# Two graph-attention layers on neighbour lists: layer 0's order on VectorE and GpSimd, its tile order, and where the prelude's transposes stand

## The chip, the cores and the metric

The kernel runs on one core of one Trainium2 chip. The metric is the device time of one execution in microseconds (us). The kernel before took 2356.4 us in the median of three runs (2355.76 to 2357.28). The profiled execution that all durations below come from took 2358.97 us, of which 2356.9 us is the span from the first to the last instruction. The engines are TensorE (PE, with its weight loads as PEld), VectorE (DVE), ScalarE (ACT), GpSimd (POOL) and SyncE (SP). Each works through its own queue in order.

## What is computed

Two graph layers over N = 2708 nodes with D = 1024 features, float32 throughout. `adj` is a symmetric 0/1 matrix with ones on the diagonal, of which a row has some 16 ones in the mean.

```python
# layer 0
f, g   = x @ Wf + bf, x @ Wg + bg
e      = relu(f @ g.T)
att    = softmax(where(adj > 0, e, -9e15), axis=1)
x      = layernorm(x + att @ (x @ W + bW))
# layer 1
h      = x @ W1
e      = leaky_relu(h @ a1 + (h @ a2).T, 0.2)
att    = softmax(where(adj > 0, e, -9e15), axis=1)
x      = layernorm(x + relu(att @ h))
```

## The kernel before

**Lists in place of the matrix.** Only the neighbours of a node enter its softmax. So the kernel first turns each row of `adj` into a list of at most 40 neighbours. It sorts the nodes by the length of their lists, in steps of four, and then works on 85 groups of 32 nodes. A group has a fixed number of tiles (`TILES`, 10 for the first and 3 for the last ones, 405 in all). In a tile each of the 128 partitions holds the feature row of one neighbour: partition 32q + i belongs to node i of the group, and q runs over four neighbours. Four groups make a block of 128 nodes, and there are 22 blocks (b0 to b21). If the lists were longer than the tiles allow, a second, dense path at the end would run (`general_path`); with these inputs it is skipped.

**Algebra.** Layer 0 doesn't form g. With M = Wf Wg^T, F = x M + c is formed for each block, and a score is the dot product of a row of F with a neighbour's row of x, plus a term q of the node itself. After the softmax the rows of x are summed (`sums`, PSUM tile `po`), scaled to y, and only then multiplied by W (`Wt`). The residual x is gathered into z, added, and normalised (`norm`). Layer 1's scores need two numbers a row, which layer 0 forms by two dots with u1b and u2b (the "u dots") when it closes a block. The row, with the second number, is scattered to a table T1 (rows of 1028 floats), and stored to X1S.

**Prelude.** For each of 22 row blocks `lists(b)` loads `adj` (1.35 MB, SP queue, pool `adjp`, four buffers), converts it on ScalarE, multiplies it by a descending index on GpSimd, and takes the largest elements on VectorE (`max`, `match_replace`). Between these, the generator `weights()` loads rows of Wf, Wg and W1 (pool `stage`, five buffers), transposes them on TensorE (`turned`), copies them out of PSUM on ScalarE, and forms M in two halves of 512 columns, then rb (for q) and u1b, u2b. Each `next(steps)` runs it up to the next `yield`, one row block of a weight. The calls after `lists(1)`, `lists(2)` and `lists(3)` run 16 of the 24 steps; the eight for W1 come after all lists. All this is in order on each engine's queue. Then the lists' lengths are ranked with VectorE and TensorE, which yields `idq` and `ids`, the indices of list rows and of x rows.

**Layer 0.** It is written out by hand in the order of the queues: `InOrder` ties each engine's instructions to the order of the program text, and records them all at L53, its own line. A `Unit` is the tiles handled at a time. A block whose tiles fit the ring of 20 slots of 128 x 1024 floats is one unit (b5 to b21: 20 tiles each in b5 to b11, 16 in b12 to b18, 12 in b19 and b20, 3 in b21); b0 to b4 have two units of two groups each. For a unit u and the next one:

1. `replicate` copies rows of F for the next block out of PSUM to all four quarters of a tile Fr (ScalarE, four copies a group).
2. `sums(u)`: TensorE forms the softmax denominators (`pt<-rs,stack`) and then `po`, tile after tile in order of t. Each tile that is done frees a ring slot, and `gathers()` then issues, on GpSimd, the gathers of later tiles as long as their slots are free, strictly in the order of `u.tiles`. Hooks within `sums` finish the close of an older block (its T1 scatter).
3. TensorE, in its order: the transposes of x for block b + 2 (`x_turn`), the product of y of block b - 1 with Wt (`Wp`), the product F of block b + 2 (`f_product`), and the transposes of y of block b.
4. GpSimd: the x rows of the residual (z) and of block b + 3 (`load_x`, one buffer xb), and four gathers of list rows.
5. VectorE: the `dots` of the next unit, one instruction for each tile as its row lands, the q dot of block b + 3 (`q_dot`, reads xb), the `soft` of the next unit (some 16 small instructions with one exp on ScalarE), and the first part of `close(b - 1)`: z added to the product, norm, and then the u dots.

For blocks of one unit (`u.only`) three quarters of the dots come first, then q_dot and the close up to the norm, then the last quarter, soft, and the u dots. `q_spread`, a matmul that spreads q over the partitions and its read on VectorE, stands in `sums`. PSUM tiles `pt` have two buffers, `pm` (Wp and F) two, `po` one. The tiles of a unit are in order of group in layer 0 (`cut(R0, False)`), in order of t in layer 1 (`cut(R1, True)`).

**Layer 1** gathers from T1 into 27 slots and needs no dots; it is otherwise alike.

Of the kernel before, what the change touches and what calls it, by code (L numbers as in the profile page):

```python
# [88 lines left out]
def listed_path(ctx, tc, x, adj, Wf, bf, Wg, bg, W, bW, W1, a1, a2, out):  # L89
# [74 lines left out]
    with tc.tile_pool(name="pre", bufs=1) as pre:  # L164
# [41 lines left out]
        with tc.tile_pool(name="adjp", bufs=4) as adjp, tc.tile_pool(name="cands", bufs=2) as cands, \  # L206
                tc.tile_pool(name="wt", bufs=1) as wt, tc.tile_pool(name="stage", bufs=5) as stage:
# [23 lines left out]
            def weights():  # L231
# [17 lines left out]
                for k in range(KC):  # L249
                    turned(Wf, k, WfT[:, :, k * P:(k + 1) * P])  # L250
                    yield
                for h in range(H):
                    half = slice(h * 512, (h + 1) * 512)
                    WgT = wt.tile([P, KC, 512], F32, name="WgT")
                    for k in range(4):
                        turned(Wg, 4 * h + k, WgT[:, :, k * P:(k + 1) * P])
                        yield
                    for k in range(KC):
                        pm = ps_m.tile([P, H, 512], F32, name="pm")
                        for i in range(KC):  # L260
                            nc.tensor.matmul(pm[:, 0, :], WfT[:, i, k * P:(k + 1) * P], WgT[:, i, :],  # L261
                                             start=(i == 0), stop=(i == KC - 1))
                        nc.scalar.copy(M[:, k, half], pm[:, 0, :])  # L263

                    pm = ps_m.tile([P, H, 512], F32, name="pm")
                    for i in range(KC):
                        nc.tensor.matmul(pm[0:64, 0, :], bfc[:, i:i + 1].to_broadcast([P, 64]), WgT[:, i, :],
                                         start=(i == 0), stop=(i == KC - 1))
                        nc.tensor.matmul(pm[64:128, 0, :], bgc[:, i:i + 1].to_broadcast([P, 64]),
                                         WfT[:, i, half], start=(i == 0), stop=(i == KC - 1))  # L270
                    crow = pre.tile([1, 512], F32, name="crow")
                    nc.scalar.copy(crow, pm[0:1, 0, :])
                    row_parts(lambda t: nc.gpsimd.dma_start(t, crow.rearrange("o (p k) -> o p k", p=P)),
                              c3[:, half])
                    nc.scalar.copy(rb[64:128, half], pm[64:128, 0, :])
                    for q in range(2):
                        nc.scalar.copy(rb[32 * q:32 * q + 32, half], pm[64 + 32 * q:96 + 32 * q, 0, :])
                for h in range(H):
                    half = slice(h * 512, (h + 1) * 512)
                    W1T = wt.tile([P, KC, 512], F32, name="WgT")  # L280
                    for k in range(4):
                        turned(W1, 4 * h + k, W1T[:, :, k * P:(k + 1) * P])
                        yield

                    pm = ps_m.tile([P, H, 512], F32, name="pm")
                    for i in range(KC):
                        for j in range(2):
                            nc.tensor.matmul(pm[64 * j:64 * j + 64, 0, :],
                                             ac[:, i, j:j + 1].to_broadcast([P, 64]), W1T[:, i, :],
                                             start=(i == 0), stop=(i == KC - 1))  # L290
                    for j, u in enumerate((u1b, u2b)):
                        mine, other = 64 * j, 64 - 64 * j
                        nc.scalar.copy(u[mine:mine + 64, half], pm[mine:mine + 64, 0, :])
                        for q in (0, 32):
                            nc.scalar.copy(u[other + q:other + q + 32, half], pm[mine + q:mine + q + 32, 0, :])

# [36 lines left out]
            for b in range(NB):  # L333
                lists(b)
                for _ in range({1: 8, 2: 4, 3: 4}.get(b, 0)):
                    next(steps)
# [102 lines left out]
    def norm(z, n):  # L439
# [17 lines left out]
        dve.tensor_scalar(sh[:n], mv[:n, 0:1], r[:n], -1.0, op0=ALU.mult, op1=ALU.mult)  # L457
        act.activation(z[:n, :D], z[:n, :D], AF.Identity, bias=sh[:n], scale=r[:n])
# [4 lines left out]
    def cut(most, in_turn):  # L463


        units, at = [], 0
        for b in range(NB):
            gs = list(range(Q * b, min(Q * b + Q, NG)))
            whole = sum(TILES[g] for g in gs) <= most
            parts = [gs] if whole else [gs[:2], gs[2:]]  # L470
            for i, p in enumerate(parts):
                u = Unit()
                u.b, u.gs, u.at = b, p, at
                u.first, u.last, u.only = i == 0, i == len(parts) - 1, whole
                u.lo, u.hi = 32 * (p[0] - Q * b), 32 * (p[-1] - Q * b) + 32
                u.G, u.T = len(p), max(TILES[g] for g in p)
                u.tiles = [(k, g, t) for k, g in enumerate(p) for t in range(TILES[g])]
                if in_turn:
                    u.tiles.sort(key=lambda m: m[2])
                u.sc = scores[len(units) % 2][:, :u.G, :u.T]  # L480
                assert len(u.tiles) <= most
                at += len(u.tiles)
                units.append(u)
        return units

    class Layer:
# [16 lines left out]
        def gathers(self):  # L503
            while self.next < len(self.order) and (self.next < self.count or self.next - self.count in self.free):
# [27 lines left out]
        def sums(self, u, po, ahead, hooks):  # L532

# [8 lines left out]
            ahead()  # L542
# [39 lines left out]
    with ExitStack() as s0s:  # L582
# [4 lines left out]
        z = new_pool("zp", 1).tile([P, TW], F32, name="z")  # L587
        units = cut(R0, False)
        lay = Layer(units, [ring], D, x, stp)
        by_block = {b: [u for u in units if u.b == b] for b in range(NB)}  # L590
        xb, q, qd, F, Fr, xTs, yTs, Wp, y = {}, {}, {}, {}, {}, {}, {}, {}, {}
# [15 lines left out]
        def q_spread(b):  # L607
            n = nrows[b]
            pt = ps_t.tile([P, 4, P], F32, name="pt")
            pe.matmul(pt[:, 0, :Q], rep[:n], qd.pop(b)[:n], start=True, stop=True)  # L610
            q[b] = small.tile([P, Q], F32, name="q")
            dve.tensor_scalar(q[b], pt[:, 0, :Q], s0, None, op0=ALU.add)

        def x_turn(b):
            xTs[b] = tp.tile([P, KC, P], F32, name="xT")
            for _ in turn(xb.pop(b), nrows[b], xTs[b]):
# [21 lines left out]

        def close(b):

            n = nrows[b]
            dve.tensor_add(z[:n, :D], flat(Wp.pop(b))[:n], z[:n, :D])
            norm(z, n)
            m = nsize[b]
# [4 lines left out]
            yield  # L649
            scatter(T1[:, :], ids[:m, b:b + 1], z[:m])  # L650

        act.dma_start(Wt, W.rearrange("(k p) d -> p k d", p=P))
        load_lists(0)
        dve.tensor_scalar(SL0, SL[:, 0:Q, :], float(N - 1), None, op0=ALU.min)
        load_x(0)
        pool.memset(z[:, D:], 0.0)
# [3 lines left out]
        for b in (0, 1):  # L660
            q_dot(b)
            q_spread(b)
            x_turn(b)
            load_x(b + 1)
            f_product(b)
            if b == 0:
                for k in range(Q):
                    replicate(0, k)
        load_lists(3)
        dots(units[0], 0, len(units[0].tiles))  # L670
        q_dot(2)
        soft(units[0])
        closing = iter(())
        for k, u in enumerate(units):
# [11 lines left out]
            for r in reps[:3]:  # L686
                replicate(b + 1, r)
            lay.sums(u, po, lambda: q_spread(ahead) if u.first and ahead is not None else None,
                     {8: [lambda s=closing: [None for _ in s]]})
            closing = iter(())  # L690
            act.activation(y[b][u.lo:u.hi], flat(po)[u.lo:u.hi], AF.Copy, scale=u.ri[u.lo:u.hi])
            if u.first:
                if back is not None:
                    gather(pool, z[:nrows[back], :D], x, ids[:nrows[back], back:back + 1])
                if ahead is not None:
                    x_turn(ahead)
                if back is not None:
                    Wp[back] = product(nrows[back], yTs.pop(back)[0], Wt, 32)
# [11 lines left out]
            if u.first and b + 3 < NB:  # L710
                load_x(b + 3)
            if u.first and b + 4 < NB:
                load_lists(b + 4)
            count = len(nxt.tiles) if nxt is not None else 0
            part = count * 3 // 4 if u.only else count
            if nxt is not None:
                dots(nxt, 0, part)
            if u.last and b + 3 < NB:
                q_dot(b + 3)
            if nxt is not None and not u.only:  # L720
# [4 lines left out]
            if nxt is not None and u.only:  # L725
                dots(nxt, part, count)
                soft(nxt)
            if back is not None:
                next(closing)
        for _ in closing:  # L730
            pass
        b = NB - 1
        gather(pool, z[:nrows[b], :D], x, ids[:nrows[b], b:b + 1])
        for _ in yTs[b][1]:
            pass
        Wp[b] = product(nrows[b], yTs.pop(b)[0], Wt, 32)
        for _ in close(b):
# [3 lines left out]
    with ExitStack() as s1s:  # L741
# [5 lines left out]
        units = cut(R1, True)  # L747
# [30 lines left out]
        def close1(b):  # L778
# [5 lines left out]
            norm(z, m)  # L784
# [7 lines left out]
        for k, u in enumerate(units):  # L792
# [9 lines left out]
            lay.sums(u, po, lambda: None, {6: [lambda s=closing: [None for _ in s]]})  # L802
# [405 lines left out]
```

## Time and profile before

| stage | us | PE busy | DVE busy | ACT busy | POOL busy | DMA share | GB/s |
|---|---|---|---|---|---|---|---|
| prelude, 0 to 239 | 239 | 185.8 | 160.1 | 110.9 | 150.8 | 0.55 | 192 |
| start of layer 0, 239 to 318 | 79 | 38.6 | 29.6 | 20.1 | 40.5 | 0.48 | 166 |
| b0 to b4, two units each, 318 to 630 | 312 | 269.6 | 229.4 | 106.5 | 175.3 | 0.65 | 218 |
| b5 to b10, 20 tiles, 630 to 1001 | 371 | 262.2 | 220.1 | 123.4 | 180.3 | 0.55 | 185 |
| b11 to the end of layer 0, 1001 to 1573 | 572 | 433.8 | 307.3 | 195.7 | 231.3 | 0.48 | 164 |
| layer 1, 1573 to 2357 | 784 | 603.0 | 228.6 | 77.1 | 430.1 | 0.76 | 273 |
| profiled execution: span 2356.9, run 2358.97 | | 1793.0 | 1175.1 | 633.7 | 1208.3 | | |

The rows are stretches of the same span, so their lengths add up to it; the busy times are those within each stretch. A line of a timeline further down gives the start in us, the busy time in us, the engine, the line of the program (L53 is the helper that records the hand-written order), the operation, output<-input with their shapes, the count, and in brackets the idle time of the engine just before and what ended it. A line of the waits gives who waited for whom, the total in us, how many times, and the longest.

### The profile page before, as it was taken

The numbers are of one execution on the slowest core, as the hardware profiler recorded it, in microseconds if no ns is written. First come the engines' busy times: TensorE is split into PE (matmuls) and PEld (weight loads), VectorE is DVE, ScalarE is ACT, GpSimd is POOL, SyncE is SP. The second block draws the span as 40 slices with busy tenths as digits, with TensorE's granted clock in tenths as the row PEclk, the third lists the DMA queues.
The fourth block names the chain that finished last, engine by engine and source line by source line (L and its number), as shares of the span: only waits on it lengthen the run. The fifth ranks groups of instructions, "written<-read, shape, count | busy, mean of one in ns | idle before, by whom it ended". The sixth has DMA issues, their size and how long they took to land. (4 is left out here: it accounts for less than half of the span.)

```text
span 2356.9 us, 22380 instructions
## 1 busy us (share of the span) xinstructions
PE 1793.0 (76%) x6982; PEld 702.8 (30%) x6982; DVE 1175.1 (50%) x3615; ACT 633.7 (27%) x769; POOL 1208.3 (51%) x1173
## 2 busy tenths in 40 slices
PE   5987469999767776677777778835687888888896
PEld 3343223333222322223333333311222322333332
DVE  3994176777756666555655555321123323333333
ACT  4553322333423332234434333100001001111111
POOL 6891647555344444554555543026566656666521
PEclk8998689999888888888888889967899988899998
DMA  8561647766455555554555554338788989888830
GB/s 291 186 216 60 237 142 241 234 220 224 142 181 189 199 196 183 176 200 167 173 176 188 182 176 159 125 138 324 262 309 299 335 313 314 296 310 306 289 151 23
DMA packets 154201, 502.94 MB, mean 213 GB/s; under 512 B 36550, under 2 KB 36550, under 8 KB 151364
## 3 DMA queue, kind: packets, MB, share of 16 engines
q0 software_dynamic: 132160, 428.47, 52.4%
q1 hardware_dynamic: 13658, 68.30, 8.0%
q10 hardware_dynamic: 8254, 4.65, 0.7%
q8 instruction: 57, 0.93, 0.2%
q14 instruction: 72, 0.59, 0.1%
HBM read 509.64 MB, written 33.75 MB: 231 GB/s over the span
## 5 line engine op out<-in xcount | busy, mean ns | idle before, releaser
L53 POOL DMA_INDIRECT ring<-in_x_dram,SL x405 | 470.5, 1162 | 551.8 <-PE po L53 413.6
L53 DVE SCALAR_TENSOR_TENSOR j<-ring,Fr 128x1024 bf16<-128x1024 f32 x405 | 496.6, 1226 | 190.5 <-DMA ring<-in_x_dram,SL 156.5
L53 PE MATMUL po<-ring,st 128*32 128x512 f32 x2820 | 474.6, 676 | 3.0 <-issue 2.5
L53 POOL DMA_INDIRECT ring<-T,SL x300 | 298.6, 995 | 190.3 <-PE po L53 79.0
L53 PE MATMUL pm<-M,yT 128*128 128x512 f32 (+1 forms) x704 | 344.4, 626 | 57.2 <-issue 54.9
L53 ACT COPY Fr<-pm 32x1024 f32<-32x1024 f32 x340 | 341.1, 1003 | 21.0 <-issue 16.5
L53 PE MATMUL pm<-M,xT 128*128 128x512 f32 (+1 forms) x704 | 320.5, 607 | 8.7 <-issue 8.7
L53 PE MATMUL pm<-Wt,xT 128*128 128x512 f32 (+1 forms) x704 | 316.2, 602 | 6.4 <-ACT xT L53 6.4
L53 PE MATMUL pt<-rs,stack 128*32 128x1 f32 x340 | 13.2, 191 | 346.7 <-DVE rs L53 158.9
L53 PEld LDWEIGHTS po<-ring,st 128*32 128x32 f32 x2820 | 120.9, 123 | 304.3 <-issue 300.6
L53 PEld LDWEIGHTS pm<-M,yT 128*128 128x128 f32 (+1 forms) x704 | 131.8, 193 | 267.3 <-issue 266.7
L53 ACT ACTIVATE z<-z,sh,rstd 128x1024 f32<-128x1024 f32 (+2 forms) x44 | 54.3, 1235 | 580.3 <-DVE sh L53 564.8
L53 ACT ACTIVATE y<-po,ri 128x1024 f32<-128x1024 f32 (+2 forms) x50 | 55.6, 1112 | 574.2 <-remote 488.5
L53 PEld LDWEIGHTS pm<-M,xT 128*128 128x128 f32 (+1 forms) x704 | 129.5, 189 | 174.8 <-issue 174.8
L53 PEld LDWEIGHTS pm<-Wt,xT 128*128 128x128 f32 (+1 forms) x704 | 127.9, 187 | 168.0 <-issue 161.2
L53 DVE TENSOR_SCALAR scores<-ring,f1q 128x2 f32<-128x2 f32 (+6 forms) x105 | 24.6, 253 | 241.1 <-DMA ring<-T,SL 210.5
L53 POOL DMA_INDIRECT more<-T,SL x105 | 105.3, 1003 | 66.7 <-PE po L53 28.8
L310 POOL TENSOR_TENSOR adj<-adj,iota 128x2708 f32<-128x2708 f32 (+1 forms) x22 | 129.8, 5936 | 15.6 <-ACT adj L309 15.5
L53 DVE SCALAR_TENSOR_TENSOR j<-xb,rb 128x1024 bf16<-128x1024 f32 (+1 forms) x22 | 26.9, 1225 | 204.1 <-DMA xb<-in_x_dram,ids 141.0
L313 DVE MAX8 cand<-adj 128x8 f32<-128x136 f32 (+2 forms) x440 | 105.7, 284 | 30.8 <-POOL adj L310 30.8
L261 PE MATMUL pm<-WgT,WfT 128*128 128x512 f32 x256 | 116.0, 614 | 6.1 <-ACT M L263 3.8
L53 PEld LDWEIGHTS pt<-rs,stack 128*32 128x32 f32 x340 | 9.6, 126 | 361.9 <-ACT xT L53 252.8
(171 smaller groups left out, 1509.7 us busy)
## 6 DMA issues: line engine op xcount, KB each, us to landing
adj<-in_adj_dram SPq DMA_DIRECT2D x21, 1354.0 KB
X1S<-z SPq DMA_DIRECT2D x21, 512.0 KB
x<-X1S SPq DMA_DIRECT2D x21, 512.0 KB
ring<-in_x_dram,SL POOLq DMA_INDIRECT x405
ring<-T,SL POOLq DMA_INDIRECT x300
rows<-in_L_gnn_Wf_dram SPq DMA_DIRECT2D x8, 512.0 KB
rows<-in_L_gnn_Wg_dram SPq DMA_DIRECT2D x8, 512.0 KB
rows<-in_L_gnn_W_dram SPq DMA_DIRECT2D x8, 512.0 KB
```

Source lines behind the costliest of these rows:

```text
L53: made = self.tc.keep_in_program_order(op(*args, **kwargs))
L261: nc.tensor.matmul(pm[:, 0, :], WfT[:, i, k * P:(k + 1) * P], WgT[:, i, :], start=(i == 0), stop=(i == KC - 1))
L310: nc.gpsimd.tensor_tensor(k[:n], k[:n], iota[:n], op=ALU.mult)
L313: nc.vector.max(cand[:n, s, :], k[:n, s * SEG:min((s + 1) * SEG, N)])
```

## The change

In the prelude the transposes of Wg's second half and of W1's first half stand in the middle of the products for M (after k = 3) instead of after them, with two buffers for a transposed half (`halfT`); `adjp` goes from four buffers to three and `stage` from five to four; the weights' rows are requested earlier in SP's order.

```diff
-        with tc.tile_pool(name="adjp", bufs=4) as adjp, ...
-                tc.tile_pool(name="wt", bufs=1) as wt, tc.tile_pool(name="stage", bufs=5) as stage:
+        with tc.tile_pool(name="adjp", bufs=3) as adjp, ...
+                tc.tile_pool(name="wt", bufs=1) as wt, tc.tile_pool(name="stage", bufs=4) as stage:
...
+                def half_turned(w, h):
+                    t = wt.tile([P, KC, 512], F32, name="halfT", bufs=2)
+                    for k in range(4):
+                        turned(w, 4 * h + k, t[:, :, k * P:(k + 1) * P])
+                        yield
+                    return t
+                WgT = yield from half_turned(Wg, 0)
                 for h in range(H):
...
                         nc.scalar.copy(M[:, k, half], pm[:, 0, :])
+                        if k == 3:
+                            nxt = yield from half_turned(*((Wg, 1), (W1, 0))[h])
...
+                    if h == 0:
+                        W1T = yield from half_turned(W1, 1)
...
-                for _ in range({1: 8, 2: 4, 3: 4}.get(b, 0)):
+                for _ in range({0: 8, 1: 4, 2: 4, 8: 4, 15: 4}.get(b, 0)):
```

In layer 0 the tiles are sorted by t within pairs of groups; all dots of the next unit stand together, then soft, then the close up to the norm; the q dot, ScalarE's z and the u dots come at the beginning of the next turn, ahead of the next dots. The gather of xb goes before that of z; q_spread's matmul moves behind the Wt product, and its read on VectorE behind the dots. The last block's z goes to a free ring slot instead of the one z tile.

```diff
-                if in_turn:
-                    u.tiles.sort(key=lambda m: m[2])
+                u.tiles.sort(key=lambda m: (m[0] // turns, m[2]))
...
+        def load_residual(b):
+            z = zs if b + 1 < NB else lay.slots[lay.next % lay.count]
+            Z[b] = zs if b + 1 < NB else z[0][:, z[1], :]
+            gather(pool, Z[b][:nrows[b], :D], x, ids[:nrows[b], b:b + 1])
...
-            for r in reps[:3]:
+            for r in reps[:1]:
                 replicate(b + 1, r)
-            lay.sums(u, po, lambda: q_spread(ahead) if u.first and ahead is not None else None,
-                     {8: [lambda s=closing: [None for _ in s]]})
+            next(closing, None)
+            if loaded is not None:
+                q_dot(loaded)
+                loaded = None
+            next(closing, None)
+            for r in reps[1:3]:
+                replicate(b + 1, r)
+            lay.sums(u, po, {12: [lambda s=closing: [None for _ in s]]})
...
+            if u.first and ahead is not None:
+                x_turn(ahead)
+            if u.first and b + 3 < NB:
+                load_x(b + 3)
+                loaded = b + 3
+            if back is not None:
+                load_residual(back)
+                Wp[back] = product(nrows[back], yTs.pop(back)[0], Wt, 32)
+            spreading = iter(())
+            if u.first and ahead is not None:
+                spreading = q_spread(ahead)
+                next(spreading)
...
-            part = count * 3 // 4 if u.only else count
             if nxt is not None:
-                dots(nxt, 0, part)
-            if u.last and b + 3 < NB:
-                q_dot(b + 3)
-            if nxt is not None and not u.only:
+                dots(nxt, 0, len(nxt.tiles))
+            for _ in spreading:
+                pass
+            if nxt is not None:
                 soft(nxt)
             if back is not None:
                 closing = close(back)
                 next(closing)
-            if nxt is not None and u.only:
-                dots(nxt, part, count)
-                soft(nxt)
```

At the start of layer 0 the x rows of block 0 are gathered before the lists, eight ring gathers go before the x rows of block 1, only two groups of F are replicated before x of block 1 is turned, and the dots of the first unit come before the q dot of block 1.

```diff
         act.dma_start(Wt, W.rearrange("(k p) d -> p k d", p=P))
+        load_x(0)
         load_lists(0)
+        q_dot(0)
...
+        lay.gathers(8)
+        x_turn(0)
+        for _ in q_spread(0):
+            pass
+        load_x(1)
         lay.gathers()
...
+        f_product(0)
+        replicate(0, 0)
+        replicate(0, 1)
+        x_turn(1)
         load_lists(3)
+        f_product(1)
+        replicate(0, 2)
+        replicate(0, 3)
         dots(units[0], 0, len(units[0].tiles))
-        q_dot(2)
+        q_dot(1)
+        load_x(2)
+        for _ in q_spread(1):
+            pass
         soft(units[0])
```

Layer 1 calls the same helpers with `cut(R1, Q)`, which gives the order it had.

## The prediction

> **What bounds the kernel now.** I read the slices first, then the waits, then timelines of one block of each kind. Three stages: prelude (0 to 239 us), layer 0 (239 to 1573), layer 1 (1573 to 2357). In layer 1 the diff changes no order (all its units already sort by t, norm() is run through), so I leave its 784 us alone. The waits, in us in total, times, longest:
>
> ```profile
> PE pt L53 <- DVE rs L53: 158.9, 16, 16.7
> DVE j L53 <- DMA xb<-in_x_dram,ids: 141.0, 10, 36.6
> PE pt L53 <- ACT xT L53: 125.4, 11, 20.8
> DVE eq L359 <- PE pt L353: 28.6, 1, 28.6
> ```
>
> TensorE waits for a unit's softmax (rs, and the xT copy queued on ScalarE behind its exp), and VectorE for xb, the x rows of a later block that no dot of this block needs. In the prelude VectorE waits once for TensorE. A block of 20 tiles in one unit (b9 to b10) on TensorE, then VectorE:
>
> ```profile
> 873.08 0.29 PE L53 MATMUL pt<-rs,stack 128*32 128x1 f32 x8 [11.97 <-ACT xT L53]
> 915.49 1.04 PE L53 MATMUL pt<-ident,y 128*128 128x128 f32 x8
> 937.38 0.29 PE L53 MATMUL pt<-rs,stack 128*32 128x1 f32 x8 [20.85 <-ACT xT L53]
> ```
>
> ```profile
> 920.02 1.23 DVE L53 SCALAR_TENSOR_TENSOR j<-xb,rb 128x1024 bf16<-128x1024 f32 x1 [9.88 <-DMA xb<-in_x_dram,ids]
> 921.42 1.22 DVE L53 TENSOR_TENSOR z<-pm,z 128x1024 f32<-128x1024 f32 x1
> 927.05 0.21 DVE L53 TENSOR_SCALAR sh<-mv,rstd 128x1 f32<-128x1 f32 x1
> 927.18 1.22 DVE L53 SCALAR_TENSOR_TENSOR j<-ring,Fr 128x1024 bf16<-128x1024 f32 x1
> 933.51 0.18 DVE L53 TENSOR_TENSOR scores<-scores,q 128x20 f32<-128x20 f32 x1
> 937.06 0.17 DVE L53 TENSOR_REDUCE rs<-scores 128x4 f32<-128x20 f32 x1
> ```
>
> TensorE has done its block by 916.5 and idles 20.9 us. VectorE had 15 dots done at 910.1, waited 9.9 for xb, did q_dot (1.4) and the close of an older block (5.8), and only then the last 5 dots (6.3) and the softmax (3.9). Gathers could not start sooner: all 20 ring slots belong to this unit and come free as its sums run. The next block's on GpSimd, first, second, last:
>
> ```profile
> 942.01 0.99 POOL L53 DMA_INDIRECT ring<-in_x_dram,SL  x1 [21.87 <-PE po L53]
> 944.80 0.99 POOL L53 DMA_INDIRECT ring<-in_x_dram,SL  x1 [1.80 <-PE po L53]
> 975.68 0.99 POOL L53 DMA_INDIRECT ring<-in_x_dram,SL  x1 [0.30 <-issue]
> ```
>
> A 16-tile block is idle too, a two-unit block (b3) hardly:
>
> ```profile
> 1266.51 1.04 PE L53 MATMUL pt<-ident,y 128*128 128x128 f32 x8
> 1280.74 0.28 PE L53 MATMUL pt<-rs,stack 128*32 128x1 f32 x8 [13.19 <-DVE rs L53]
> ```
>
> ```profile
> 523.01 7.13 PE L53 MATMUL pm<-Wt,xT 128*128 128x512 f32 x16
> 530.08 0.23 PE L53 MATMUL pt<-rs,stack 128*32 128x1 f32 x4
> 560.40 0.23 PE L53 MATMUL pt<-rs,stack 128*32 128x1 f32 x4 [4.13 <-DVE rs L53]
> ```
>
> **The sum, against the profiled span of 2356.9 us** (0.5 above the median of the runs, 2356.4). Intervals run from rs matmul to rs matmul.
>
> *20-tile blocks, b5 to b11.* Six intervals, 629.92 to 1001.06, 61.9 each. Afterwards q_dot, the close and the two u dots stand after the softmax, ahead of the next dots: 5.8+1.4+2.5+0.2 = 9.9 us, and VectorE's old first dot came 9.4 after rs (946.76), when its row landed. So they hide behind the first gather. Twenty dots at 1.27 (25.4) then end at about 35, earlier than the gathers, which decide: 9.4 to the first landing, then 19 more and two 0.5 MB transfers among them, the T1 scatter and the X1S store, which formerly fell before the gathers. Pace: 975.68-949.19 over 16 issues is 1.66; ten landings in a row (dots at 952.46 to 970.67) give 1.82; I take 1.72. Sorting by pairs frees two slots per t step instead of one, which lets the queue fill sooner; since the transfers then set the pace I count nothing more for it. 9.4 + 21x1.72 + last dot 1.3 + q 0.2 + softmax 3.9 = 50.9. TensorE's own 43.7 (937.38 to 981.11) lies below. Six times -11.0 = **-66**. b11 to b12 has 16 gathers: 43.9, TensorE 43.7, with the hand-over 44.5 for 59.3: **-15**.
>
> *16-tile blocks.* 1060.37 to 1391.52, six intervals of 55.2, and 52.3 to b19. Four slots are spare, so 12 gathers and the two transfers remain: 9.4 + 13x1.72 + 5.2 = 37. TensorE's chain is longer: 40.6 from 1226.96 to the end of the y transposes. It would gain 1.3 in the sums if there is no gap before them (48 po matmuls took 7.46 after a gap of 10.35 us and 5.34 at 1483.16 without; 64 took 8.43 here), and lose some 0.9 where the second x transposes wait for a PSUM slot until ri, now queued behind the u dots, is read; hand-over 0.3. I take 41: six times -14.2 and -11.3 = **-96**. The TensorE page of the Trainium skill ("TensorE: Matmul & The Clock Gate", Part 1) has the array at half clock after an idle window of about 3.4 us; those two rows agree in direction, and by full speed alone the interval would be 39.6.
>
> *Two-unit blocks b1 to b4.* TensorE-bound: at 530.08 the second unit's rs was ready since 521.3. Afterwards the q matmul stands behind the Wt product, and q's read on VectorE ahead of the second unit's softmax. So softmax waits for Wt: 0.6 + 0.2 + 3.4 + hand-over, about 5 us of idle TensorE. The close and the u dots then start 5 later, the 12 dots and the softmax end at about 33.5 after the first rs + 30, TensorE at 31.5: 2 us idle in place of 4.5. Net +3 each, **+12** (0 to +24). b0 and the step to b5: **-2**.
>
> *Start of layer 0* (idq 238.5 to the first rs 317.6). load_x(0) now precedes the lists, so x lands at 244.1 (it took 4.5 from issue), F(0) ends at 263.3 instead of 270.0, and two replicate groups (8.1) instead of four (16.3) stand before the next work. The dots no longer wait for q_dot(1), whose xb landed at 288.07: they run from 271.5, not 290.7. SL0 comes 1.5 later, one xb gather more is among the ring's; rows are there long before. **-19** (-12 to -22).
>
> *End.* b20 to b21, 30.4: the close of b19 (waiting 13.4 for z) leaves the chain; TensorE's 5.3+14.8+1.0 and the copy give 22.8. From b21's rs to its T1 scatter, 56.6: z of the last block has a slot of its own and the Wt product no longer follows ScalarE's z (6.4): 7+14.8+0.7+1+14.5+10.4 = 48.7. **-15**.
>
> *Prelude.* TensorE ends it (228.1 against 199.8 on VectorE). The weight transposes between the products took 12.9 (115.7 to 128.6) and 10.8 (193.8 to 204.6), waiting mostly for ScalarE copies; inside M I estimate 8.5 and 4.5, as the copies still share ScalarE's queue with the adjacency blocks: -11. Wf's copies now run through before the second adjacency block: M starts some 7 earlier. VectorE has then 28.6 of slack to lose: adjp has three buffers, and on SP the last W1 rows wait for stage buffers that are freed by transposes in the middle of M, with blocks 16 to 21 queued behind. I put the lists' end at 205 instead of 196. **-18** (-24 to 0).
>
> Sum: -66-15-96+12-2-19-15-18 = -219, so a span of 2138 and a run at **2137 us**.
>
> **Rivals.**
> *Gathers faster.* If 1.30 (issue to issue, as from 973.06 to 978.27) is the pace, 20-tile blocks fall to TensorE's 44: another -41, 2096. Against: ten landings at 1.82. Chance 0.10.
> *Gathers slower.* 16-tile rows from 1182.02 to 1193.55 go at 1.92. Then 55 per 20-tile block, +25; others stay with TensorE: 2162. 0.13.
> *The close in front delays the block.* u dots wait for z on ScalarE, z for a replicate group (4.06); ri, the second x transposes and the dots wait behind. If a hand-over of 5 stays in each of 13 whole intervals: +65, 2202. For: the prelude and two-unit blocks show such in-order waits. Against: 9.4 us of gather latency as cover. 0.13.
> *VectorE holds up GpSimd.* If each gather issue waits for one dot, 0.99+1.23+0.30 = 2.52 a gather, 20-tile blocks grow to 67.7 and 16-tile ones become 47: about 2290. Against: from 484.74 to 489.92 five gathers beside unbroken dots take 0.99 each. 0.03. "SBUF — State Buffer" of the Trainium skill (Who interferes with whom) says so of a VectorE instruction with two SBUF inputs against a GpSimd one that reads SBUF; those rows speak against a price here.
> *Slower: transfers collide.* X1S, T1, z, xb and the ring's now fall into one shorter stretch. With p us a transfer, layer 0's whole intervals sum to 234p-610 against before and the rest to -42: no gain from p = 2.79, 2407 at 3.0. For: layer 0 never moved over 240 GB/s in 100 us. Against: layer 1's gathers run at 321 GB/s, 1.64 each. 0.04.
> *The prelude part does nothing*, as the lists take TensorE's place: 2155, inside the forecast's own range.
>
> **How the numbers follow.** Forecast 0.56, its own range 2108 to 2175. The range 2095 to 2202 takes in the faster and slower pace and half of the third rival. A difference under 0.2% (5 us) could not be told from none; only a sum of several rivals lands there, 0.01. Slower 0.04, faster 0.95.
>
> **What would show it.** In whole blocks j<-xb,rb after the softmax with no wait; 20-tile intervals near 51 with VectorE waiting for ring rows to the end; 16-tile ones near 41 with TensorE's gap before rs gone; in b1 to b4 a new TensorE gap of 5 us after Wt; eq's wait for pt below 10 us; layer 1 unchanged at 784. Wrong if the gap before rs stays over 10 us in 16-tile blocks, or if a gather takes over 2.5.

## The result and the profile after

The changed kernel took 2123.24 us in the median of four runs (2115.4 to 2125.75). The kernel before, run beside it, took 2356.08 (2349.6 to 2357.28). The ratio is 0.9011, 95% interval 0.8981 to 0.9041. The profiled run took 2115.4 us with a span of 2113.6, so all stages below add up to -243.3 against the profile of before (2356.9).

The waits of the changed kernel (who waited for whom, us in total, times, longest), those that answer to the ones shown of before:

```profile
PE pt L53 <- DVE rs L53: 36.5, 9, 5.6
PE pt L53 <- ACT xT L53: 24.1, 19, 11.7
DVE q L53 <- remote: 86.6, 10, 15.4
DVE j L53 <- DMA xb<-in_x_dram,ids: 5.7, 2, 5.5
DVE eq L365 <- PE pt L359: 1.1, 1, 1.1
```

TensorE's waits for the softmax have gone from 158.9 + 125.4 to 36.5 + 24.1, and VectorE's for xb from 141.0 to 5.7. One wait is new: VectorE for q. `eq` no longer waits for TensorE, but that brought nothing, as the table shows.

| stage, from the traces | before | after | measured | predicted |
|---|---|---|---|---|
| prelude, to idq | 238.5 | 242.0 | +3.5 | -18 |
| idq to the first rs | 79.1 | 63.7 | -15.4 | -19 |
| b0 to b4 (to b5's rs) | 312.4 | 314.9 | +2.5 | +10 |
| b5 to b10, six intervals | 371.1 | 259.4 | -111.7 | -66 |
| b11 to b18, eight intervals | 442.7 | 338.2 | -104.5 | -111 |
| b19 to b21's rs | 69.7 | 60.7 | -9.0 | -7 |
| b21's rs to layer 1's first rs | 91.2 | 80.8 | -10.4 | -8 |
| layer 1 from there | 752.2 | 753.8 | +1.6 | 0 |

(The prediction's -15 for the end is split here as -7 and -8, its -15 for b11 and -96 for the 16-tile blocks are joined, and so are +12 and -2 for b0 to b4.)

A block of 20 tiles in the changed kernel (b8 to b9), on TensorE, VectorE and GpSimd, three timelines:

```profile
750.50 0.21 PE L53 MATMUL pt<-rs,stack 128*32 128x1 f32 x5 [2.55 <-ACT xT L53]
...
791.55 1.04 PE L53 MATMUL pt<-ident,y 128*128 128x128 f32 x8
794.30 0.21 PE L53 MATMUL pt<-rs,stack 128*32 128x1 f32 x5 [1.71 <-ACT xT L53]
```

```profile
750.18 0.17 DVE L53 TENSOR_REDUCE rs<-scores 128x4 f32<-128x20 f32 x1
...
756.01 1.22 DVE L53 SCALAR_TENSOR_TENSOR j<-xb,rb 128x1024 bf16<-128x1024 f32 x1
...
759.95 1.22 DVE L53 SCALAR_TENSOR_TENSOR j<-ring,Fr 128x1024 bf16<-128x1024 f32 x1
...
788.83 1.24 DVE L53 SCALAR_TENSOR_TENSOR j<-ring,Fr 128x1024 bf16<-128x1024 f32 x1
790.00 0.21 DVE L53 TENSOR_SCALAR q<-pt,s 128x4 f32<-128x4 f32 x1
```

```profile
753.82 0.99 POOL L53 DMA_INDIRECT ring<-in_x_dram,SL  x1 [5.20 <-PE po L53]
...
783.61 0.99 POOL L53 DMA_INDIRECT ring<-in_x_dram,SL  x1 [0.30 <-issue]
```

The close, the q dot (756.01, with no wait ahead of it) and the u dots stand behind rs, and the first dot still comes 9.5 us after the rs matmul, as it did before (9.4). Its row no longer sets it: in b6 to b10 VectorE starts the first dot without a wait, straight after its own 8.9 to 9.5 us of work. The 20 dots then run to the end with few gaps: 759.95 to 788.83 is 28.9 us for 19 steps, 1.52 a row. TensorE ends its block at 792.6 and waits 1.7 us: the two engines are close to balanced.

### The profile page after: what moved, and what is told of

Its sections match the earlier page's. It is cut to its first block, busy times and chain, and to the rows that moved or that the text cites. A ratio compares the mean times of both kernels' runs of the same rounds, so it can differ in the third digit from the quotient of the medians.

```text
span 2113.6 us, 22443 instructions
## 1 busy us (share of the span) xinstructions
PE 1771.2 (84%) x6982; PEld 702.9 (33%) x6982; DVE 1177.4 (56%) x3615; ACT 635.7 (30%) x769; POOL 1173.8 (56%) x1174
## 3 DMA queue, kind: packets, MB, share of 16 engines
q0 software_dynamic: 132160, 428.47, 57.3%
## 5 line engine op out<-in xcount | busy, mean ns | idle before, releaser
L53 POOL DMA_INDIRECT ring<-in_x_dram,SL x405 | 434.2, 1072 | 356.9 <-PE po L53 160.5
L53 PE MATMUL po<-ring,st 128*32 128x512 f32 x2820 | 448.9, 629 | 4.4 <-issue 3.8
L53 PE MATMUL pm<-M,yT 128*128 128x512 f32 (+1 forms) x704 | 351.7, 634 | 63.1 <-issue 59.9
L53 ACT ACTIVATE scores<-scores 128x20 f32<-128x20 f32 (+7 forms) x50 | 10.7, 214 | 479.4 <-DVE scores L53 419.9
L319 DVE MAX8 cand<-adj 128x8 f32<-128x136 f32 (+2 forms) x440 | 105.7, 286 | 59.8 <-POOL adj L316 59.6
L265 PE MATMUL pm<-halfT,WfT 128*128 128x512 f32 x256 | 116.6, 612 | 8.4 <-ACT M L267 8.4
L53 POOL DMA_INDIRECT SL<-LD,idq x85 | 86.6, 1019 | 25.9 <-issue 24.7
L53 DVE TENSOR_TENSOR st<-scores,stack 128x640 f32<-128x640 f32 (+7 forms) x50 | 35.3, 707 | 105.4 <-issue 48.8
```

What stands on the lines that cost most here:

```text
L53: made = self.tc.keep_in_program_order(op(*args, **kwargs))
L319: nc.vector.max(cand[:n, s, :], k[:n, s * SEG:min((s + 1) * SEG, N)])
```

## Experiments

Three sets were run, each beside runs of the kernel before: it took 2355.9 us in the first set, 2257.5 in the second, 2352.8 in the third. In the second set transfers were faster (in the last quarter of the span a fortieth of it moved up to 396 GB/s, in the two others up to 329), so times are compared within a set, or as a ratio to before.

### The prelude as before (first set)

The whole prelude of the kernel before, under the changed layer 0.

> The changed kernel (2123 in the median) with the whole prelude as it was before: transposes between the halves of M, adjp 4, stage 5, the old order of the weights' rows. My prediction's term (the prelude part is worth 18 us): 2141, with layer 0's idq some 18 later than the changed kernel's. The rival (the lists have taken TensorE's place, the part is worth nothing): 2118 to 2126, idq within 3 us of the changed kernel's.

Measured 2122.1 us, ratio 0.9002 (0.8973 to 0.9031), idq at 239.0 against 242.0. The prelude's part is worth nothing; the rival holds.

### W1's last rows later (second set)

```diff
-                for _ in range({0: 8, 1: 4, 2: 4, 8: 4, 15: 4}.get(b, 0)):
+                for _ in range({0: 8, 1: 4, 2: 4, 8: 4, 20: 4}.get(b, 0)):
```

> The changed kernel with W1's last four row blocks requested after the adjacency block 20 instead of after 15. Theory A (on SP the last adjacency blocks queue behind these requests, which wait for stage buffers until the middle of M's second half, and the lists end 25 us late): the lists end near 205, idq comes 12 to 20 us earlier than in the changed kernel, 2103 to 2112. Theory B (the lists are held up by ScalarE's and GpSimd's order beside the transposes, not by SP): idq within 4 us of the changed kernel's, 2118 to 2128.

Measured 1985.2, ratio 0.8774 (0.8728 to 0.8821). The three other kernels of this set have the changed kernel's prelude, and their idq is at 243.2 to 245.0; here it is at 234.3. So at idq 9 us come from moving four requests in one queue. In the whole time that is 6.8 us against the nearest kernel of this set (1992.0, the pair order for 20 tiles alone); the changed kernel itself did not run in it. SP's queue in the changed kernel, then in this one:

```profile
152.47 10.40 SPq L53 DMA_DIRECT2D rows<-in_L_gnn_W_dram  x4
163.00 34.93 SPq L53 DMA_DIRECT2D adj<-in_adj_dram  x6
```

```profile
178.62 2.42 SPq L53 DMA_DIRECT2D rows<-in_L_gnn_W_dram  x4
184.74 0.36 SPq L53 DMA_DIRECT2D adj<-in_adj_dram  x1
```

Four requests that took 10.4 us (they waited for stage buffers that transposes in the middle of M free) now take 2.4, and the last adjacency block is requested at 184.7 instead of up to 198. What ends the prelude is read off VectorE's `eq`: in the changed kernel, here, and with the old prelude:

```profile
230.92 0.41 DVE L365 TENSOR_TENSOR eq<-eq,pt 128x242 f32<-128x242 f32 x1 [1.05 <-PE pt L359]
```

```profile
223.64 0.41 DVE L365 TENSOR_TENSOR eq<-eq,pt 128x242 f32<-128x242 f32 x1 [8.80 <-PE pt L359]
```

```profile
228.64 0.41 DVE L359 TENSOR_TENSOR eq<-eq,pt 128x242 f32<-128x242 f32 x1 [29.02 <-PE pt L353]
```

With the old prelude VectorE has 29.0 us to spare and TensorE sets the end; with the change VectorE's lists and TensorE end together, over 2 us later than before; with the rows requested later TensorE is the bound again, 5 us earlier than before. Theory A holds in kind, at less than its size: the lists end at 211.2 for its 205, and TensorE's own chain stands right behind.

### The close back among the dots (first set)

```diff
+            part = count * 3 // 4 if u.only else count
             if nxt is not None:
-                dots(nxt, 0, len(nxt.tiles))
+                dots(nxt, 0, part)
+            if back is not None and u.only:
+                closing = close(back)
+                next(closing)
+            if nxt is not None:
+                dots(nxt, part, count)
```

(The later `close` remains for blocks of two units.)

> The changed kernel with the close up to the norm put back between the first three quarters and the last quarter of the dots for blocks of one unit; q_dot stays where the change put it. Theory A (the close's 5.8 us stood on the path from the last rows to the softmax): 20-tile intervals go from 43.2 to 48 or 49 and 16-tile ones by up to 4, in sum 2160 to 2190. Theory B (only the wait for xb was on the path, and the close fits into VectorE's waits for rows): 2118 to 2130.

Measured 2284.5, ratio 0.9694 (0.9666 to 0.9723): 161 us of the change's 233 go with this one edit, far more than either theory gave. b5 to b10 take 58.3 us each instead of 43.2, b11 to b18 50.8 instead of 42.3. VectorE, then TensorE, in one 20-tile block of it:

```profile
960.37 1.22 DVE L53 TENSOR_TENSOR z<-pm,z 128x1024 f32<-128x1024 f32 x1 [8.11 <-DMA z<-in_x_dram,ids]
```

```profile
972.61 1.12 PE L53 MATMUL pt<-ident,y 128*128 128x128 f32 x4 [11.26 <-DVE q L53]
976.33 0.29 PE L53 MATMUL pt<-rs,stack 128*32 128x1 f32 x8 [2.61 <-ACT xT L53]
```

The close costs not only its 5.8 us of work. z is gathered behind all ring rows of the next unit and behind xb (issued at 954.72, used at 960.37), so the close waits 8.1 us for it with five dots queued behind. And q, whose PSUM slot the y transposes need, is read only after those dots, at 972.34: TensorE waits 11.3 us in the middle of the block. No run puts the q dot alone back in front of the softmax, so what the wait for xb was worth by itself is read from the waits, not tested.

### The close moved alone (third set)

The kernel before, with all dots together, then q dot, softmax, and then the close and the u dots for blocks of one unit:

```diff
-            part = count * 3 // 4 if u.only else count
+            part = count
...
-            if nxt is not None and not u.only:
+            if nxt is not None:
                 soft(nxt)
...
-            if nxt is not None and u.only:
-                dots(nxt, part, count)
-                soft(nxt)
```

> The kernel before with one part of the change alone: in blocks of one unit all dots stand together, then the q dot, the softmax, and only then the close and the u dots. Theory A (it was the close with its wait for z, ahead of the last quarter of the dots, that set the softmax; undoing it cost the changed kernel 161 us): 20-tile blocks near 50, 16-tile ones near 44 to 48, 110 to 150 us less than the kernel before. Theory B (the wait for xb, which the q dot still meets ahead of the softmax, keeps the most of it): 20 to 60 us less.

Measured 2310.4, ratio 0.9815 (0.9769 to 0.9862): 42 us. A 20-tile block takes 57.3 us, a 16-tile one 52.9 (60.6 and 54.4 in the kernel before, profiled beside it). The size is theory B's, but the reason is mostly another. ScalarE, then TensorE, at the end of one block:

```profile
915.80 1.24 ACT L53 ACTIVATE z<-z,sh,rstd 128x1024 f32<-128x1024 f32 x1 [6.73 <-DVE sh L53]
917.07 1.07 ACT L53 COPY xT<-pt 128x512 f32<-128x512 f32 x2
```

```profile
917.70 0.29 PE L53 MATMUL pt<-rs,stack 128*32 128x1 f32 x8 [17.95 <-ACT xT L53]
```

VectorE had rs ready at 910.0 (its wait for xb ahead of the q dot was only 1.5 here). But on ScalarE the z of the close stands ahead of the copies that free the PSUM slot for rs, and it waits for the norm until 915.8. So rs lies ready for 7.7 us: what the close no longer takes on VectorE it takes on ScalarE. The other 10.2 of TensorE's 17.95 passed before rs was ready; the 20 gathers of this block, in order of group, go at 1.82. In the change a new `yield` in `norm` puts ScalarE's z into the next turn:

```diff
         dve.tensor_scalar(sh[:n], mv[:n, 0:1], r[:n], -1.0, op0=ALU.mult, op1=ALU.mult)
+        yield
         act.activation(z[:n, :D], z[:n, :D], AF.Identity, bias=sh[:n], scale=r[:n])
```

My prediction named the move of ScalarE's z only as a possible delay. That this line is a condition of the gain follows from the 7.7 us here; no run takes it alone out of the changed kernel.

### Order of group again (first set)

```diff
-        units = cut(R0, 2)
+        units = cut(R0, 1)
```

> The changed kernel with layer 0's tiles in order of group again, not of t within pairs of groups. Theory A (the pair order frees two slots a step, so that gathers go without pauses; this is what my prediction counted at nothing, and it makes the 43.2 us of a 20-tile block): 20-tile intervals of 48 to 51 us with pauses of 1.6 to 1.8 between the first gathers, 2155 to 2180. Theory B (the order on VectorE alone makes it): 20-tile intervals of 43 to 44, 2118 to 2128.

Measured 2119.2, ratio 0.9003 (0.8979 to 0.9027), no difference in sum, but two that cancel. b5 to b10 take 47.5 us each instead of 43.2 (+25.3 in six); b11 to b18 take 323.1 instead of 338.2, and b0 to b4 311.5 instead of 314.9. The waits of GpSimd for TensorE, in the changed kernel and in this one:

```profile
POOL ring L53 <- PE po L53: 222.0, 62, 24.7
```

```profile
POOL ring L53 <- PE po L53: 239.5, 98, 23.4
```

In order of group one slot comes free a step, and GpSimd waits more often; in 20-tile blocks its first gather leaves 3.7 to 4.0 us after rs instead of 2.2 to 4.0, and its 20 gathers go at 1.52 to 1.81 instead of 1.46 to 1.57 (first to last issue over 19). So the pair order, which I counted at nothing, is worth 4.3 us a 20-tile block. Theory A holds there; the total is in theory B's range. What it costs elsewhere is in the last section.

### q's matmul ahead of the Wt product (first set)

```diff
-            if back is not None:
-                load_residual(back)
-                Wp[back] = product(...)
             spreading = iter(())
             if u.first and ahead is not None:
                 spreading = q_spread(ahead)
                 next(spreading)
+            if back is not None:
+                load_residual(back)
+                Wp[back] = product(...)
```

> The changed kernel with q's matmul ahead of the Wt product instead of behind it; its read on VectorE stays behind the dots. Theory A (TensorE's 5.4 us before each second unit of b1 to b4 come from the place of the matmul alone): those waits fall below 1 us, a pair of units takes 56 instead of 61.3, the total is 2103; in 16-tile blocks VectorE reads q as soon as its dots are done. Theory B (in ten blocks of the changed kernel VectorE read q 2.4 to 2.9 us after GpSimd's last indirect DMA of a burst, however long ago the matmul ran; the burst holds the read up): the reads stay 2.4 to 2.9 us behind the end of the burst, the 5.4 us stay, and the total is 2118 to 2126.

Measured 2226.7, ratio 0.9445 (0.941 to 0.9479): 103 us slower than the changed kernel; both theories missed the size. In b1 to b4 TensorE's waits before the second units are gone, as theory A has it, but waits of 2.6 to 4.4 before q's matmul and, but for b1, of 2.6 to 2.7 before the first units stand in their place. Theory B falls: q is read there with 6 to 9 us of GpSimd's burst still to run. What costs the 103 us stands in the other blocks. TensorE, then ScalarE, in a 16-tile block:

```profile
989.98 0.66 PE L53 MATMUL pt<-ident,xb 128*128 128x128 f32 x4 [0.57 <-DVE ri L53]
997.13 0.59 PE L53 MATMUL pt<-qd,rep 128*128 128x4 f32 x2 [6.49 <-issue]
```

```profile
987.34 8.12 ACT L53 COPY Fr<-pm 32x1024 f32<-32x1024 f32 x8
995.49 1.11 ACT L53 ACTIVATE y<-po,ri 128x1024 f32<-128x1024 f32 x1
996.50 1.06 ACT L53 COPY xT<-pt 128x512 f32<-128x512 f32 x2
```

q's matmul needs one of the two `pt` slots, which hold x's transposes until ScalarE has copied them, behind eight replicate copies and y. (The profile names the 6.49 "issue"; that it ends within the two copies that start at 996.50 shows what it is.) In the changed kernel the 14.8 us of the Wt product lie over this time. The place behind Wt, for which the prediction charged 5 us in each two-unit block, is what keeps 20- and 16-tile blocks (51.5 and 49.2 here) at TensorE's pace.

### List rows every second block (second set)

Eight gathers of list rows in the turns of odd blocks and none in even ones, to see what q's read waits for.

```diff
-            if u.first and b + 4 < NB:
-                load_lists(b + 4)
+            if u.first and b % 2:
+                for c in (b + 3, b + 4):
+                    if c > 3 and c < NB:
+                        load_lists(c)
```

> The changed kernel with the gathers of list rows issued eight at a time in the turns of odd blocks and none in those of even ones, instead of four in each. Theory A (while GpSimd issues indirect DMAs without a pause, what waits for TensorE's semaphore goes on only 2.4 to 2.9 us after the burst): in b1 and b3 the burst ends 5.2 us later, q is read some 7 us after its matmul instead of 2, and TensorE waits 10 to 11 before the second units instead of 5.4; in b2 and b4 it ends 5.2 earlier and TensorE waits 3 to 4. Theory B (the 2 us are a latency of the matmul's own): q is read 2 us after its matmul in all of them, and the waits stay at 5.4.

One profiled run took 1996.5. In b1 to b4 q is read 0.3 us after its matmul, in even blocks and in odd ones, and in b1 while GpSimd's burst still runs (matmul 393.28, read 393.60, burst to 397.61). So neither theory holds in this set: the 2 us are no latency of the matmul, and a burst alone doesn't make them. As the changed kernel itself wasn't profiled in this set, the edit can't be parted from the faster transfers.

### Pair order for 20 tiles alone, and q read later (second set)

```diff
-                u.tiles.sort(key=lambda m: (m[0] // turns, m[2]))
+                step = turns if turns == Q or len(u.tiles) == most else 1
+                u.tiles.sort(key=lambda m: (m[0] // step, m[2]))
```

> The changed kernel with the pair order only for units of 20 tiles and the order of group for all others. By the traces of the two orders: 43.2 a block for b5 to b10 as in the changed kernel, 39.8 to 41 for 16-tile blocks and 30.3 with 28.4 to 29.4 for two-unit blocks as in order of group: 2095 to 2102. The rival (what b5 to b10 gain by the pair order is given back in the blocks behind, whose gathers start from another state): 2112 to 2125.

The second kernel has this edit and one more:

```diff
-            for _ in spreading:
-                pass
+            if u.only:
+                for _ in spreading:
+                    pass
             if nxt is not None:
                 soft(nxt)
+            for _ in spreading:
+                pass
```

> The last kernel, and in two-unit blocks VectorE reads q behind the second unit's softmax instead of ahead of it (q is wanted two blocks later). Theory A (the second unit's softmax waits for the Wt product only by this place of the read): TensorE's waits before the second units of b0 to b4 fall from some 3 to 5 us to below 1, 12 to 20 us less than the kernel before it, 2078 to 2090. Theory B (another wait ends as late, the rows or the close of the block before): less than 5 us.

Measured 1992.0 (0.8817, 0.8773 to 0.886) and 1987.9 (0.88, 0.8755 to 0.8846). Here all kernels have 39.8 us for most 16-tile blocks, the one with the pair order throughout too, so the first edit had nothing to win; its expected totals had been worked out from the slower first set. The second takes 6.2 us from b0 to b4 (309.5 to 303.3) and 4.1 from the whole. First units of b1 to b4, which took between 30.3 and 31.9 us, take 28.1; second ones of b1 to b3, between 28.4 and 29.2, take some 30.0. The wait that the prediction saw (softmax behind q behind Wt, 3.8 to 4.0 us here) is gone, and TensorE waits 3.6 to 3.9 us for rs before the next first unit instead of 0.3 to 0.9, as theory B has it.

### The three edits together, beside both kernels (third set)

> The changed kernel as it is, as the measure for the others: where the kernel before takes 2356, the prediction's case, 2116 to 2126 (ratio 0.90). In the last runs the kernel before took 2257 and layer 1's gathers moved up to 396 GB/s instead of 321; there the one look at a kernel near this one took 1996 (0.884). Theory A (the change takes away waits for rows as well as for VectorE, so faster transfers leave less to gain): ratio above 0.90 where before takes 2257. Theory B (what it takes away is the order, whose waits stand whatever the transfers do, and the blocks behind it are bound by TensorE): 1994 to 2002 there, ratio 0.88 to 0.89.

> The changed kernel with three edits together: the pair order only for units of 20 tiles, q read behind the softmax in two-unit blocks, and W1's last rows requested after adjacency block 20. If they add up (each was measured beside the others: some 4, 6 and 10 us), 12 to 22 us less than the changed kernel run beside it. The rival (the prelude's 10 us are taken back by the start of layer 0, whose first gathers then wait for the list stores): less than 8 us.

> The kernel before as it is, for its trace beside the changed kernel's on the same chip. Where its time is 2356, the stages of the first profile within 1%. Where it is 2257: theory A (the faster transfers shorten the waits for rows) 20-tile blocks below 58 instead of 61.9, layer 1 some 80 shorter; theory B (the difference is all in layer 1) 61 to 62 and 54 to 55 in the blocks of layer 0 as before.

The changed kernel took 2137.6 (0.9058, 0.9006 to 0.911), the three edits together 2078.7 (0.8851, 0.879 to 0.8912), 58.9 us less than the changed kernel, by the medians 2.8%, where 12 to 22 were expected. This is the best of all versions in a set where it ran beside both kernels. Before, with 2347.3 in its profiled run, has 60.6 us for a 20-tile and 54.4 for a 16-tile block, 1.6 to 2% below the first profile (61.9 and 55.3), where 1% was expected; that set does not tell the theories on faster transfers apart, since its transfers were the slower ones. By the two profiles, 64.0 us apart, idq is 6.5 us earlier in the combination than in the changed kernel beside it, b0 to b4 take 7.4 less, b5 to b10 21.0 less, b11 to b18 22.2 less (most 16-tile blocks 39.8), and layer 1, which no edit touches, 7.0 less. The blocks b5 to b18 give more than I expected because the changed kernel itself lost time there in this set: its b9 and b10 took 48.0 and 59.1 us instead of 43, and its 2137.6 lies above the expected 2116 to 2126. What the edits give without that loss is not shown.

## Why the prediction came out right

The predicted 2137 is 0.7% above the measured 2123, inside the range; by the spans it is 2138 against 2113.6 (the profiled run is the fastest of its four). The main steps held as put, two sizes missed, in opposite directions.

**What held.** VectorE's wait for xb and the close inside the dots were what set the 20- and 16-tile blocks (the close by the run that puts it back, the wait for xb by the waits alone), and behind rs they leave the first dot where it was: 9.5 us after rs, q dot without a wait. That they hide below the first gather is only about right. The first gather now leaves 2.2 us after rs in most blocks, and in b5, where VectorE does wait for its row, gather and dot are 4.5 us apart; so the row could be there at some 6.7 (an estimate from these two), and VectorE's 8.9 to 9.5 us stand over it. TensorE's chain of 42.1 in the block shown leaves that little room to cost anything, so the third rival, that the close in front delays the block by 5 us, fell.

16-tile blocks went to TensorE's chain: 39.8 where undisturbed, for a predicted 41 (338.2 in eight for some 331). The gain in the sums came too: 64 po matmuls took 7.05 us behind a gap of 0.3, and 8.43 before. Full speed alone, which the prediction set beside "TensorE: Matmul & The Clock Gate" of the Trainium skill (Part 1), would have made 39.6; the granted clock of b17 and b18, at 39.8 each, is 1.00, and that of b12 to b17 was 0.87 before. TensorE waits 5.4 us ahead of second units in b1 to b4, predicted "about 5"; per block of two units it came to +1.4 instead of +3. The start and the end came within 4.5 us of their terms; no run tests these two alone. (Two slips in the working change little: the terms of the last stretch, behind b21's rs, add up to 48.4, not 48.7, and the third rival counts 13 whole intervals where its neighbour's formula has 14.)

**The term that was too small: 20-tile blocks, -111.7 for -66.** The step was "Pace: ... I take 1.72". I put 21 transfers at 1.72 behind the first landing; measured, the last dot starts 28.9 us after the first, which is 1.38 for each of the 21. Issue to issue the gathers go at 1.46 to 1.57 on average in these blocks. The 1.66 and 1.82 that I chose from came out of single stretches of before, where the six 20-tile blocks span 1.44 to 1.78. I also counted the pair order at nothing "since the transfers then set the pace": it is worth 4.3 of the 7.7 us a block by which the forecast was high, as the order of group shows. The rival "gathers faster", with its fall to TensorE's 44, describes what happened, at 1.38 instead of its 1.30. The sign that the forecast gave for these blocks, VectorE waiting for rows to the end near 51, did not show.

**The term that was wrong: the prelude, +3.5 for -18.** The step was "I put the lists' end at 205 instead of 196". It ended at 226.9. I had named the mechanism (W1's last rows waiting on SP with blocks 16 to 21 behind them) and given it 9 us. In the trace these requests hold SP for 10.4 us, the blocks come late, VectorE's wait for GpSimd's `adj` grows from 30.8 to 59.6 us, and ScalarE's queue, which carries the lists' `PL` and the weights' copies in one order, hands lateness back to TensorE (6.59 and 6.06 us of waits for halfT copies; the second copy stands behind a `PL` that waits 6.35 for VectorE). Putting the old prelude back left the time the same, and asking for those rows later brought idq 9 us forward. This was the last of the prediction's rivals, and it came true. TensorE's own part was too large as well. In the changed kernel the second half of M starts 15.1 us earlier (113.56 for 128.63), but the first product with W1 only 9.5 earlier (195.09 for 204.60), after a wait of 7.48 for ScalarE's copy of M. With the lists out of the way, in the run with the later rows, `eq` comes 5 us earlier than with the old prelude, not 18.

The errors were +21 for the prelude and -46 for the pace; with the smaller ones they add up to -24. That the total is so near is in part luck, since they have opposite signs.

## What to carry to other kernels

When an engine does a block's work in order, put first what the next engine waits for, and put behind it all that waits for a transfer issued last; then follow the moved step's instructions on every other queue too, for one of them left in its old place can give much of the gain back (ScalarE's z held a ready rs for 7.7 us in the block shown). An instruction placed late can be there because something else covers its wait for a buffer: look which slot it takes before moving it forward. Take the pace of a transfer from whole blocks, not from the stretch at hand.

## What the hardware showed that I had not expected

**TensorE paused, and its results were late, while GpSimd issued gathers.** In b10 of the changed kernel's run in the third set (TensorE's timeline):

```profile
862.77 0.67 PE L53 MATMUL pm<-Wt,xT 128*128 128x512 f32 x1 [0.73 <-issue]
...
874.11 1.01 PE L53 MATMUL pm<-Wt,xT 128*128 128x512 f32 x1 [1.09 <-issue]
...
880.47 0.58 PE L53 MATMUL pm<-rows,ones 3*128 3x512 bf16 x1 [1.23 <-issue]
```

Matmuls that by the profile wait for nothing come 1.4 to 2.8 us apart for some 18 us, where 0.43 is usual, while 27 indirect DMAs are issued back to back (842.44 to 878.56). The block took 59.1 us. In the first profile of the changed kernel b15 has one such pause, of 1.67 us at 1081.47, and VectorE's read of q is late:

```profile
1083.71 0.22 DVE L53 TENSOR_SCALAR q<-pt,s 128x4 f32<-128x4 f32 x1 [6.42 <-remote]
```

q's matmul had run at 1071.82; its reader went on 11.9 us later, 2.8 us after GpSimd's last DMA of the burst ended at 1080.94. In all ten waits for q of that profile the read comes 2.4 to 2.9 us after the end of such a burst. That is no rule: with q's matmul ahead of the Wt product the reads in b1 to b4 are 1.8 to 4.0 us late, with 6 to 9 us of the burst still to run.

Late reads of this kind number ten to twelve in the profiles of the changed kernel and of the one with the old prelude (first and third set). There are two with the order of group (b12 and b18), three with the three edits together (b12, b16 and b18, 7.4 to 9.7 us after the matmul's end), and none in the second set with its faster transfers. TensorE's "issue" waits between 300 and 1350 us are 13.3 us in the changed kernel's first profile (another 7.3 under that name is a wait for rs) and 36.3 in its second, 9.9 and 5.6 in those of before, 0.8 with the order of group under the change, and at most 0.3 in the second set. So it is strongest with the pair order, in which gathers run on without a pause from the sums to the list rows, and it did not show with the faster transfers. But before has the order of group and pauses too, so neither is shown to be the condition; which resource is held is not settled, and whether the 2 us in two-unit blocks are the same thing neither. Leaving pair order to the 20-tile blocks lessened it in the one set where this could be seen: of the 16-tile blocks b12 to b18 one is longer (b12, 43.5 us).

**The same program, two speeds of memory.** Before took 2355.9, 2257.5 and 2352.8 us in the three sets. The record names a different chip for each set (2, 0 and 10); whether the chip is the reason no run shows, and before itself was not profiled in the second set. Layer 1 has the same instructions in all the changed kernels. In the second set a fortieth of the span moves up to 394 to 396 GB/s in the last quarter, at most 329 in the two others, and from its first rs to the end layer 1 takes 661.7 to 664.7 us instead of 747.2 to 754.6. That is some 90 of the 98 us by which before was faster in that set.
